# A two-layer graph network on one core: the Newton step of the layer norm on ScalarE, attention emitted earlier, the mean row spread a pair later, one table loaded in disjoint pieces

## The chip, the core and the metric

The kernel runs on one core of a Trainium2 chip. Everything is fp32. The metric is the device time of one execution in microseconds, the median of several. Five engines work side by side, each through its own queue in order, and semaphores hold them together: TensorE (PE; its weight loads PEld), VectorE (DVE), ScalarE (ACT), GpSimd (POOL) and SyncE (SP, which here only issues DMAs). GpSimd issues the indirect DMAs, the gathers and scatters.

## The reference

`x` has 2708 rows of 1024 features; `adj` is a sparse 0/1 matrix of 2708 x 2708 whose first rows have the most ones.

```python
# layer 0
q, k, v = x @ Wq.T + bq, x @ Wk.T + bk, x @ Wv.T + bv
z = (q @ k.T) / sqrt(1024) * adj
z = where(z == 0, -10000, z)
out0 = relu(softmax(z, axis=1) @ v)
x = layernorm(x + out0)            # (t - mean) / sqrt(var + 1e-5)
# layer 1
x = layernorm(x + adj @ (x @ W1) + b1)
```

## The kernel before

**Sparse attention.** Scores are computed at the neighbours of a row only. A first stage (0 to about 134 us) transposes weights, forms M from Wq and Wk, so that a score is x_j . y_i with y = x M, and lists each row's neighbours from `adj`. The rows are then sorted by their number of neighbours into 22 blocks of 128 rows. A record of 28 words a row (neighbours, degree, number of the row) goes through DRAM to the tile `tabs`. The rows of the first 8 blocks (`FAMILY = 8`) are sorted and recorded first, those of the others later. Block 0 holds the rows with most neighbours. The neighbours of its first 32 rows (`HUB`) are dealt over all partitions as shares of a table of their own (the "hub"); its partitions 0 to 31, free by that, take a second share of the neighbours of rows 32 to 63. So `tab0` is block 0's table with 128 records, of which the first 32 rows are overwritten by columns of the next 32 records. `records_out` (L754-772) writes the records and issues these loads on GpSimd's queue: L769, L770, L771, L772.

**The y pairs** (about 134 to 434 us). y for two blocks at a time is formed as seven half products of 8 matmuls each (`half_products`, L308-316) instead of eight, from sums and differences of the operands, in the manner of Strassen. GpSimd forms the sums of x (`y_sums_of`, L395-403, its first is L398). Parts of one pair and the next alternate (`y_pair`, L442).

**Attention** goes on VectorE beside the products: `attend` and `attend_shares` gather neighbour rows of x into a ring of buffers (`gather_slot`, L530, tile `g`), multiply and sum them with y (`score`, L1066), do a running softmax, and sum the rows weighted into `r` (L1125, L1202). For the hub the shares must be joined: a transpose of the maxima (L1210) and a product (L1220) on TensorE.

**The order is partly written out, partly budgeted.** The list `steps` (L1285) has the y steps, then the first layer-0 pair, the step "mean", and nine more pairs. `ahead(i)` (L1396-1436) is called before each step. It finishes what is pending and adds the step's estimated free VectorE time to `credit`: 8.9 for a y step of one block (`HALF_PAIR`), other values from `COST`. While the credit is positive it emits attention jobs from the list `jobs`, each of which draws it down. Within an engine the framework's scheduler then orders the instructions by priority and dependence; `follow` adds a dependence by hand, and evictions of products (`add`, L327-332) have a high priority.

**Layer-0 pairs** (about 434 to 747 us). `turn_pair` (L1232-1245) transposes the two blocks' `r` (`flip`, L978, transposes L985, copies L986) and forms four sums `s_all` on VectorE (L1241-1244). `project_pair` (L1250) multiplies by Wv in seven half products, with bias added at the eviction (L332). `finish_pair` (L1260-1273) applies relu, adds x, and normalizes: `norm` (L1020-1042) does the sum of squares (L1028), logarithm (L1031) and exponential (L1033) on ScalarE, one Newton step for the inverse root on VectorE (L1035, L1036, L1038), minus mean times root (L1040), and then applies both on ScalarE (L1041). `norm_halves` (L1044-1060) is the variant for the last block of a layer. `scatter` (L971-976) writes the rows to `x1_d`. The tiles `t` have two buffers for each place.

**The mean.** The last two blocks, 20 and 21, hold rows without neighbours; their softmax is uniform, so all of them get the mean of x times Wv. `project_mean` (L1003-1018) multiplies, copies four quarters (`quarters`) and spreads them to all partitions by eight matmuls (L1014) into two banks of `p_o`, which the half products use too; `finish0` (L1156-1167) finishes these blocks after the step "mean".

**Layer 1** (about 763 us on). For each row the neighbours' rows of x1 are gathered (L530) and summed on VectorE (L1505, L1508), ten units of two blocks are multiplied by W1, and `norm` and `scatter` to `out` follow. Between the layers are 13 matmuls on data of no use (`WARM`, L1557).

In one call `norm` runs on one block, so 42 calls in a launch: 21 in each layer. The path that computes densely when a check of the lists raises `flag` isn't taken here.

Of the kernel before, what the change touches and what calls it, by code (L numbers as in the profile page):

```python
# [9 lines left out]
F32 = mybir.dt.float32  # L10
# [6 lines left out]
ALU = mybir.AluOpType  # L17
# [4 lines left out]
P = 128  # L22
# [61 lines left out]
def sparse_part(ctx, tc, x, xT, adj, wqT, wkT, wvT, bq, bk, bv, w1, b1, out):  # L84
# [28 lines left out]
    with es:  # L113
# [35 lines left out]
        nc.vector.memset(ones, 1.0)  # L149
        eps = const.tile([P, 1], F32, name="eps")  # L150
        nc.vector.memset(eps, EPS)
        xbT = const.tile([P, DC], F32, name="xbT")
        tabs = const.tile([P, NB, REC], I32, name="tabs")
        degs = const.tile([P, NB], F32, name="degs")
# [169 lines left out]
        def spare_bank():  # L324
            return p_tr.tile([P, 4, P], F32, name="tr").rearrange("p a b -> p (a b)")
# [428 lines left out]
        def records_out(f, nb, rec, pos_i, k0, k1, behind=None):  # L754
            for b in range(k0, k1):
                put = nc.gpsimd.indirect_dma_start(
                    out=tab_ds[f][:, :], out_offset=bass.IndirectOffsetOnAxis(ap=pos_i[:, b:b + 1], axis=0),
                    in_=rec[:, b, :], in_offset=None)
                if behind is not None:
                    follow(put, behind)  # L760
                tc.declare_no_dep(put.ins, group=f"tab{f}", reason="disjoint rows: positions are unique")
                tc.add_to_no_dep_group(f"tab{f}", put.ins)
            if k1 < nb:
                return
            b0 = families[f][0]
            nc.gpsimd.dma_start(out=tabs[:, b0:b0 + nb, :], in_=tab_ds[f].rearrange("(b p) e -> p b e", p=P))
            if f == 0:

                nc.gpsimd.dma_start(out=tab0, in_=tab_ds[0][:P, :])  # L769
                nc.gpsimd.dma_start(out=tab0[:HUB, :J0], in_=tab_ds[0][HUB:2 * HUB, ROW - J0:ROW])  # L770
                nc.gpsimd.dma_start(out=tab0[:HUB, :ROW - J0], in_=tab_ds[0][HUB:2 * HUB, J0:ROW])  # L771
                nc.gpsimd.dma_start(out=tab0[:HUB, ROW:], in_=tab_ds[0][HUB:2 * HUB, ROW:])  # L772
# [230 lines left out]
        def project_mean(w):  # L1003

            acc = p_o.tile([P, HALF], F32, name="po")
            column_tiles(acc, lambda c: xbT[:, c:c + 1].to_broadcast([P, HUB]), w, True)
            quarters = xb_pools[0].tile([P, D // G], F32, name="quarters", bufs=1)
            nc.scalar.copy(quarters, acc[:, :D // G])
            po = []
            for h in range(NH):  # L1010
                acc = p_o.tile([P, HALF], F32, name="po")
                for g in range(h * G // NH, (h + 1) * G // NH):
                    k = g * D // G - h * HALF
                    put = nc.tensor.matmul(acc[:, k:k + D // G], ident[:, g * HUB:g * HUB + 1].to_broadcast([P, P]), quarters,  # L1014
                                           start=True, stop=True)
                po.append(acc)
            products.append(put)
            return po

        def norm(t, sm, n, sm2=None):  # L1020

            nm = stat.tile([P, 1], F32, name="lnm")
            if sm2 is None:
                nc.vector.tensor_scalar_mul(nm[:n], sm[:n], -1.0 / D)
            else:
                nc.vector.tensor_scalar(nm[:n], sm[:n], sm2[:n], -1.0 / D, op0=ALU.add, op1=ALU.mult)  # L1026
            vs = stat.tile([P, 1], F32, name="vs")
            nc.scalar.activation(junks[:n], t[:n], AF.Square, bias=nm[:n], accum_out=vs[:n])  # L1028

            lv = stat.tile([P, 1], F32, name="lv")  # L1030
            nc.scalar.activation(lv[:n], vs[:n], AF.Ln, bias=eps[:n], scale=1.0 / D)  # L1031
            near = stat.tile([P, 1], F32, name="near")
            nc.scalar.activation(near[:n], lv[:n], AF.Exp, scale=-0.5)  # L1033
            ve = stat.tile([P, 1], F32, name="ve")
            nc.vector.scalar_tensor_tensor(ve[:n], vs[:n], D * EPS, near[:n], op0=ALU.add, op1=ALU.mult)  # L1035
            nc.vector.tensor_scalar(ve[:n], ve[:n], near[:n], -0.5 / D, op0=ALU.mult, op1=ALU.mult)  # L1036
            rstd = stat.tile([P, 1], F32, name="rstd")
            nc.vector.scalar_tensor_tensor(rstd[:n], ve[:n], 1.5, near[:n], op0=ALU.add, op1=ALU.mult)  # L1038
            nmr = stat.tile([P, 1], F32, name="nmr")
            end = nc.vector.tensor_tensor(nmr[:n], nm[:n], rstd[:n], op=ALU.mult)  # L1040
            applied.append(nc.scalar.activation(t[:n], t[:n], AF.Identity, bias=nmr[:n], scale=rstd[:n]))  # L1041
            return end

        def norm_halves(t, stats):  # L1044

# [110 lines left out]
        def finish0(b, po, xr):  # L1156
            n = rows[b]
            t = (xb_pools[0] if b == last[-1] else wa).tile([P, D], F32, name="t", bufs=2)
            for h in range(NH):
                hs = slice(h * HALF, (h + 1) * HALF)  # L1160
                with tc.high_priority(URGENT):
                    nc.vector.tensor_add(t[:n, hs], po[h][:n], bias_bc[:n, hs])
            sm = stat.tile([P, 1], F32, name="sm")
            nc.vector.scalar_tensor_tensor(t[:n], t[:n], 0.0, xr[:n], op0=ALU.max, op1=ALU.add, accum_out=sm[:n])
            end = norm(t, sm, n)
            scatter(x1_d[:, :], b, n, t, "x1")
            return end

        def attend_shares(b, got):

# [225 lines left out]
        def ahead(i):  # L1396
            nonlocal credit, pending, wv_t
            kind, b = steps[i]
            for p in pending:
                p[0](*p[1:])  # L1400
                credit -= END * (2 if p[0] is finish_pair else 1)
            pending = []
            credit += COST.get(kind, COST.get(b, HALF_PAIR))
            step[0] = i
            join(i, 3 if left_y else 1)
            if kind == "y" and b == NB - 2:
                (q11, q12), (q21, q22) = wv_q
                follow(nc.vector.tensor_sub(q12, q12, q11), products[-2])
            if kind == "p" and b == pairs[0]:
                (q11, q12), (q21, q22) = wv_q  # L1410
                wv_t = differences()
                nc.vector.tensor_sub(wv_t[0], q22, q12)
                nc.vector.tensor_sub(wv_t[1], wv_t[0], q11)
                nc.vector.tensor_sub(wv_t[2], q21, wv_t[0])
            for c in [c for st in steps[i:i + 3] for c in blocks_of(st) if not left_y and c != 0]:
                while c not in got:
                    credit -= run_job()
            while 0 in jobs and i >= steps.index(("p", (0, 7))) - 3:
                credit -= run_job()
            while jobs and i == len(steps) - 1:  # L1420
                credit -= run_job()
            while jobs and credit > 0 and (jobs[0] in running or len(ring) < RB):
                if not spread and len(jobs) <= late_jobs:
                    break
                credit -= run_job()
            if not left_y:
                turn(i)
            if kind == "y":
                if FAMILY + 1 <= b < FAMILY + 5:
                    next(deal)  # L1430
                if 6 <= b - FAMILY < 11:
                    k0 = 3 * (b - FAMILY - 6)
                    records_out(*later_records, k0, min(k0 + 3, NB - FAMILY), products[-2])
                if b == FAMILY + 11:
                    records_back(1)
                    nc.sync.dma_start(out=bias_bc, in_=bv.to_broadcast([P, D]))

        wv_t = None
        for i, (kind, b) in enumerate(steps):
# [13 lines left out]
                    xb_pools.append(xb_pool)  # L1453
                    xb_bc.append(xb_pool.tile([P, D], F32, name="xb_bc"))
            elif kind == "mean":
                po = project_mean(wv_q)
                pending = [(finish0, b_, po, gather_x(x, b_, b_ == last[-1])) for b_ in last]
            else:
                for k, b_ in enumerate(b):
                    pair_x[b_] = gather_x(x, b_, k)  # L1460
                pending = [(finish_pair, b, project_pair(b, *turned[b]))]
                if i == len(steps) - 4:
                    bcast_rows(u_bc, u_col)
                if i >= len(steps) - 3:
                    row_constants((9, 9, 5)[i - len(steps) + 3])
                if i == len(steps) - 2:
                    for b_ in single:
                        single_scores(b_)
                if b == pairs[0]:
                    bcast_rows(xb_bc[0], xbT)  # L1470
                    spread.append(b)
# [440 lines left out]
```

## Time and profile before

| | |
|---|---|
| median of three runs | 1063.62 us (1061.48, 1063.62, 1068.64) |
| the profiled execution, own time | 1064.65 us |
| its span in the trace | 1062.8 us |
| TensorE busy | 957.9 us, 2675 matmuls |
| VectorE busy | 863.9 us |
| ScalarE busy | 420.9 us |
| GpSimd busy | 600.3 us |
| moved by DMA | 229.23 MB |

"Busy" counts the time in which an engine executes something; the rest of the span it waits or issues. In lines of the waits view the columns are: engine, what waits and its line, after the arrow the engine or DMA whose result came last, then microseconds in total, times, and the longest. In lines of a timeline: start, length, engine, line, operation, number of instructions in the row, and in brackets the engine's idle time before it with what ended that. In lines of the groups view: line, engine, operation, out and in with their shapes, count, busy time, mean nanoseconds of one, and the idle time before. "L1041" is line 1041 of the kernel before.

### The profile page before, as it was taken

Reading aid. Unit: us, or ns where it says so; the run is one execution under the profiler, and the core shown is the slowest. Engines: PE = TensorE matmul, PEld = TensorE weight load, DVE = VectorE, ACT = ScalarE, POOL = GpSimd, SP = SyncE. Lnnn points to the kernel's source line nnn. Section 1 sums busy time; section 2 is a strip of 40 time slices with the busy share of each in tenths; the row PEclk is TensorE's granted clock in tenths of the full one; section 3 lists DMA queues with packets and bytes.
Section 4 is the critical chain, followed back from the end, with each engine's and each line's share of the span. In section 5 each row is a group of like instructions: output and inputs, shape, how many; then the busy total and the mean of one; then the engine's idle time right before and its main releaser. Section 6 shows DMA issues by size and latency. Waiting matters only on the chain.

```text
span 1062.8 us, 10517 instructions
## 1 busy us (share of the span) xinstructions
PE 957.9 (90%) x2675; PEld 451.1 (42%) x2675; DVE 863.9 (81%) x2035; ACT 420.9 (40%) x932; POOL 600.3 (56%) x479
## 2 busy tenths in 40 slices
PE   8889999699968999897899989997799999989894
PEld 6334344244423444353454444443344444535341
DVE  8999997587677878899889989996668877869632
ACT  4633536463342434231442454431421343352621
POOL 4841043243677784445656666783587777768510
PEclk9989999899989899898999999998899999999998
DMA  9456679346777578554844897899597599987731
GB/s 358 150 178 182 195 223 288 108 148 216 165 232 230 172 225 283 190 157 124 239 149 114 246 259 211 289 320 357 183 303 189 200 318 283 326 239 220 210 107 43
DMA packets 106093, 229.23 MB, mean 216 GB/s; under 512 B 20014, under 2 KB 47414, under 8 KB 106024
## 3 DMA queue, kind: packets, MB, share of 16 engines
q0 software_dynamic: 51152, 159.06, 49.4%
q1 hardware_dynamic: 54872, 69.42, 20.2%
q8 instruction: 23, 0.38, 0.1%
q14 instruction: 46, 0.38, 0.1%
HBM read 218.10 MB, written 33.64 MB: 237 GB/s over the span
## 4 chain that ended last, share of the span: by engine, by line
PE 29%; DVE 26%; issue 18%; DMA 14%; POOL 9%; ACT 2%; SPq 0%; POOLq 0%; DVEq 0%; ACTq 0%
PE po L310 22%; PE tr L310 5%; DVE junkv L1066 5%; POOL g L530 3%; DMA g<-x_d,tabs 3%; DVE r L1125 3%; DMA g<-in_x_dram,tabs 3%; DVE t L332 2%; DVE at_a L239 2%; DMA wv<-in_wvT_dram 2%; POOL xr L514 1%; DMA xr<-x_d,tabs 1%; DMA x_d<-t,tabs 1%; POOL g L514 1%; DMA g<-x_d,tab 1%
## 5 line engine op out<-in xcount | busy, mean ns | idle before, releaser
L310 PE MATMUL po<-t,s_all 128*128 128x512 f32 x320 | 153.4, 623 | 11.3 <-DVE xr L332 6.0
L530 POOL DMA_INDIRECT g<-in_x_dram,tabs x84 | 109.8, 1307 | 56.9 <-issue 14.2
L1066 DVE SCALAR_TENSOR_TENSOR junkv<-yg,g 128x1024 uint8<-128x1024 f32 x84 | 107.0, 1274 | 20.3 <-DMA yg<-y_d,tabs 8.9
L1508 DVE SCALAR_TENSOR_TENSOR r<-g,valid,r 128x1024 f32<-128x1024 f32 x77 | 98.2, 1281 | 18.6 <-DMA g<-x_d,tabs 15.9
L310 PEld LDWEIGHTS po<-t,s_all 128*128 128x128 f32 x320 | 62.7, 199 | 92.6 <-issue 72.0
L310 PE MATMUL po<-wv,s_all 128*128 128x512 f32 x160 | 77.4, 623 | 16.8 <-DVE s_all L1241 9.5
L530 POOL DMA_INDIRECT g<-x_d,tabs x66 | 77.4, 1173 | 24.7 <-issue 14.9
L1125 DVE SCALAR_TENSOR_TENSOR r<-g,pr,r 128x1024 f32<-128x1024 f32 x64 | 86.0, 1344 | 5.6 <-ACT r L1123 5.0
L310 PE MATMUL po<-y_t,xt 128*128 128x512 f32 x160 | 77.2, 629 | 14.8 <-DVE yo L332 14.1
L310 PE MATMUL po<-y_t,y_s 128*128 128x512 f32 x160 | 74.0, 606 | 13.0 <-POOL y_s L398 13.0
L239 DVE FIND_INDEX8 at_a<-ones,a 128x8 uint16<-128x83 f32 (+3 forms) x132 | 82.1, 630 | 0.2 <-issue 0.2
L1041 ACT ACTIVATE t<-t,nmr,rstd 128x1024 f32<-128x1024 f32 (+1 forms) x40 | 49.3, 1238 | 78.6 <-DVE nmr L1040 62.8
L1028 ACT ACTIVATE junks<-t,lnm 128x1024 uint8<-128x1024 f32 (+1 forms) x40 | 45.9, 1146 | 80.6 <-DVE lnm L1026 77.4
L310 PE MATMUL po<-w,rT 128*128 128x512 f32 x160 | 75.3, 613 | 2.6 <-DVE t L1545 2.5
L310 PE MATMUL po<-t,rT 128*128 128x512 f32 x160 | 74.5, 605 | 1.6 <-DVE t L332 1.6
L255 ACT ACTIVATE junk<-a 128x2756 uint8<-128x2756 uint32 (+1 forms) x22 | 55.0, 2502 | 45.1 <-issue 30.6
L310 PE MATMUL po<-w,s_all 128*128 128x512 f32 x160 | 72.3, 593 | 0.0
L310 PE MATMUL po<-wv,rT 128*128 128x512 f32 x160 | 71.5, 597 | 0.0
L508 ACT ACTIVATE junka<-xt 128x128 uint8<-128x128 f32 x168 | 51.8, 308 | 46.3 <-PE po L310 32.8
L986 ACT COPY rT<-tr 128x512 f32<-128x512 f32 x76 | 41.4, 584 | 70.9 <-PE tr L985 46.4
L310 PEld LDWEIGHTS po<-y_t,xt 128*128 128x128 f32 x160 | 31.8, 202 | 57.0 <-issue 37.4
L310 PEld LDWEIGHTS po<-wv,s_all 128*128 128x128 f32 x160 | 31.3, 201 | 56.4 <-issue 34.7
(415 smaller groups left out, 1904.6 us busy)
## 6 DMA issues: line engine op xcount, KB each, us to landing
xt<-in_xT_dram SPq DMA_DIRECT2D x21, 512.0 KB
y_d<-yo SPq DMA_DIRECT2D x42, 256.0 KB
a<-in_adj_dram SPq DMA_DIRECT2D x21, 413.5 KB
a<-in_adj_dram SPq DMA_DIRECT2D x21, 338.5 KB
a<-in_adj_dram SPq DMA_DIRECT2D x21, 263.5 KB
wq_i<-in_wqT_dram SPq DMA_DIRECT2D x8, 512.0 KB
wk_i<-in_wkT_dram SPq DMA_DIRECT2D x8, 512.0 KB
wv<-in_wvT_dram SPq DMA_DIRECT2D x16, 256.0 KB
```

The lines of the kernel that those rows point to most:

```text
L239: nc.vector.max_index(at[:n, i], ones[:n, :8], a[:n, cuts[i] + 8 * i:cuts[i + 1] + 8 * i + 8])
L255: put = nc.scalar.activation(junk[:n], loaded[b][:n, :AW].bitcast(U32), AF.Sign, accum_out=cnt[:n, b:b + 1])
L310: put = nc.tensor.matmul(acc, a[:, k], w[:, k], start=start and k == 0, stop=stop and k == DC // 2 - 1, skip_group_check=True)
L332: nc.vector.tensor_add(to, acc, what)
L508: put = nc.scalar.activation(junka[:, :xt.shape[2]], xt[:, c, :], AF.Copy, scale=of_first if c < DC // 2 else 1.0, accum_out=xs[:, c, b:b ...
L530: nc.gpsimd.indirect_dma_start(out=dst[:n], out_offset=None, in_=src, in_offset=bass.IndirectOffsetOnAxis(ap=at, axis=0), bounds_check=N - ...
L986: nc.scalar.copy(rT[:, g * 4:g * 4 + 4, :], tr)
L1028: nc.scalar.activation(junks[:n], t[:n], AF.Square, bias=nm[:n], accum_out=vs[:n])
L1041: applied.append(nc.scalar.activation(t[:n], t[:n], AF.Identity, bias=nmr[:n], scale=rstd[:n]))
L1066: put = nc.vector.scalar_tensor_tensor(junkv[:n], yg[:n], scale, xg[:n], op0=ALU.mult, op1=ALU.mult, accum_out=s)
L1125: nc.vector.scalar_tensor_tensor(r[:n], xg[j][:n], pr[:n, j:j + 1], r[:n], op0=ALU.mult, op1=ALU.add)
L1508: put = nc.vector.scalar_tensor_tensor(r[:n], xg[:n], ok[:n, j:j + 1], r[:n], op0=ALU.mult, op1=ALU.add)
```

## The change

Five edits.

1. Block 0's table is loaded into partitions 32 to 127 only, so that it no longer covers the 32 rows that the next loads write.
2. `norm` does its Newton step on ScalarE: four VectorE instructions are replaced by five activations with per-partition scale or bias, with two constant tiles, set once, for -0.5 eps and 1.5. The values are grouped otherwise: (-0.5/D vs - 0.5 eps) near^2 + 1.5, times near.
3. `project_mean` returns the quarters; the eight spreading matmuls are a function of their own, which is hung behind the sixth half product from there on (`between`), and write to banks from the transposes' pool instead of `p_o`. The last two blocks are finished after the pair (4, 3) instead of after "mean".
4. The credit of the last six y steps (b from 14 to 19) is 1.7 larger.
5. The return values of `norm` and `finish0`, which nothing uses, are gone.

```diff
--- before.py
+++ after.py
+        half_eps, three_halves = [const.tile([P, 1], F32, name=name) for name in ("half_eps", "three_halves")]
+        nc.vector.memset(half_eps, -0.5 * EPS)
+        nc.vector.memset(three_halves, 1.5)
...
             if f == 0:
 
-                nc.gpsimd.dma_start(out=tab0, in_=tab_ds[0][:P, :])
+                nc.gpsimd.dma_start(out=tab0[HUB:], in_=tab_ds[0][HUB:P, :])
                 nc.gpsimd.dma_start(out=tab0[:HUB, :J0], in_=tab_ds[0][HUB:2 * HUB, ROW - J0:ROW])
                 nc.gpsimd.dma_start(out=tab0[:HUB, :ROW - J0], in_=tab_ds[0][HUB:2 * HUB, J0:ROW])
                 nc.gpsimd.dma_start(out=tab0[:HUB, ROW:], in_=tab_ds[0][HUB:2 * HUB, ROW:])
...
             nc.scalar.copy(quarters, acc[:, :D // G])
+            return quarters
+
+        def spread_mean(quarters, behind):
+
             po = []
             for h in range(NH):
-                acc = p_o.tile([P, HALF], F32, name="po")
+                acc = spare_bank()
                 for g in range(h * G // NH, (h + 1) * G // NH):
                     k = g * D // G - h * HALF
                     put = nc.tensor.matmul(acc[:, k:k + D // G], ident[:, g * HUB:g * HUB + 1].to_broadcast([P, P]), quarters,
                                            start=True, stop=True)
+                    follow(put, behind, same=True)
                 po.append(acc)
-            products.append(put)
             return po
...
             nc.scalar.activation(near[:n], lv[:n], AF.Exp, scale=-0.5)
+            nc.scalar.activation(vs[:n], vs[:n], AF.Identity, bias=half_eps[:n], scale=-0.5 / D)
+            nc.scalar.activation(lv[:n], near[:n], AF.Square)
             ve = stat.tile([P, 1], F32, name="ve")
-            nc.vector.scalar_tensor_tensor(ve[:n], vs[:n], D * EPS, near[:n], op0=ALU.add, op1=ALU.mult)
-            nc.vector.tensor_scalar(ve[:n], ve[:n], near[:n], -0.5 / D, op0=ALU.mult, op1=ALU.mult)
+            nc.scalar.activation(ve[:n], lv[:n], AF.Identity, bias=three_halves[:n], scale=vs[:n])
             rstd = stat.tile([P, 1], F32, name="rstd")
-            nc.vector.scalar_tensor_tensor(rstd[:n], ve[:n], 1.5, near[:n], op0=ALU.add, op1=ALU.mult)
+            nc.scalar.activation(rstd[:n], near[:n], AF.Copy, scale=ve[:n])
             nmr = stat.tile([P, 1], F32, name="nmr")
-            end = nc.vector.tensor_tensor(nmr[:n], nm[:n], rstd[:n], op=ALU.mult)
+            nc.scalar.activation(nmr[:n], nm[:n], AF.Copy, scale=rstd[:n])
             applied.append(nc.scalar.activation(t[:n], t[:n], AF.Identity, bias=nmr[:n], scale=rstd[:n]))
-            return end
...
-            credit += COST.get(kind, COST.get(b, HALF_PAIR))
+            credit += COST.get(kind, COST.get(b, HALF_PAIR + (1.7 if kind == "y" and b >= FAMILY + 6 else 0)))
...
             elif kind == "mean":
-                po = project_mean(wv_q)
-                pending = [(finish0, b_, po, gather_x(x, b_, b_ == last[-1])) for b_ in last]
+                quarters, po = project_mean(wv_q), []
+                between[len(began) + 6] = [lambda put: po.extend(spread_mean(quarters, put))]
             else:
                 for k, b_ in enumerate(b):
                     pair_x[b_] = gather_x(x, b_, k)
                 pending = [(finish_pair, b, project_pair(b, *turned[b]))]
+                if b == pairs[1]:
+                    pending += [(finish0, b_, po, gather_x(x, b_, b_ == last[-1])) for b_ in last]
```

More of the change, by code (lines that the diff above doesn't have):

```diff
@@ L1164, in finish0 @@
             nc.vector.scalar_tensor_tensor(t[:n], t[:n], 0.0, xr[:n], op0=ALU.max, op1=ALU.add, accum_out=sm[:n])
-            end = norm(t, sm, n)
+            norm(t, sm, n)
             scatter(x1_d[:, :], b, n, t, "x1")
-            return end
         def attend_shares(b, got):
```

## The prediction

> **What bounds the kernel now.** I read the engine totals first, then the digits by slice, then the engine waits, and then the timelines at those places where TensorE stands still.
>
> ```profile
> span 1062.8 us, 10517 instructions
> PE 957.9 (90%) x2675; PEld 451.1 (42%) x2675; DVE 863.9 (81%) x2035; ACT 420.9 (40%) x932; POOL 600.3 (56%) x479
> PE   8889999699968999897899989997799999989894
> ...
> DVE  8999997587677878899889989996668877869632
> ```
>
> TensorE is busy 90% of the span, VectorE 81%. The stage view (25 us each) splits this: from 175 to 200 VectorE works 13.2 of 25 us, from 450 to 700 it works 24.9, 23.7, 24.9, 18.7, 25.0, 25.0, 24.1, 22.4, 25.0 and 25.0, and in layer 1 about 19 to 20. So in the ten layer-0 pairs two engines are nearly full at once, and a VectorE microsecond counts there; in layer 1 it doesn't. What can be won is TensorE's standing time, so I look at who ends it.
>
> ```profile
> PE po L310 <- POOL y_s L398: 13.0, 2, 10.6
> PE po L310 <- DVE s_all L1241: 9.5, 3, 5.3
> DVE t L332 <- DMA x_d<-t,tabs: 12.5, 3, 8.3
> ACT t L1041 <- DVE nmr L1040: 62.8, 22, 15.8
> POOL x_d L972 <- ACT t L1041: 33.2, 9, 6.8
> ...
> 195.92 2.07 PE L310 MATMUL po<-y_t,y_s 128*128 128x512 f32 x2 [10.61 <-POOL y_s L398]
> ...
> 447.87 2.07 PE L310 MATMUL po<-wv,s_all 128*128 128x512 f32 x2 [5.28 <-DVE s_all L1241]
> ...
> 731.55 4.79 PE L310 MATMUL po<-wv,s_all 128*128 128x512 f32 x6 [7.33 <-DVE t L332]
> ```
>
> The first five are waits (total, times, longest), the last three are TensorE's timeline with the gap ahead in brackets. One y product waits 10.61 us for GpSimd; the first pair waits 5.28 us for its second operand; the last but one stretch waits 7.33 us for an addition that itself waits for a scatter. Later gaps of the pairs, from the same timeline: 3.91, 0.77, 1.57, 4.00 (to 529.29), 0.45, 2.65.
>
> ```profile
> 183.58 0.57 POOL L769 DMA_DIRECT2D tab<-tab_d  x1
> 184.46 1.02 POOL L514 DMA_INDIRECT rec_r<-tab_d,r_i  x1 [0.30 <-issue]
> 188.49 0.55 POOL L770 DMA_DIRECT2D tab<-tab_d  x1 [3.01 <-DMA tab<-tab_d]
> 189.03 0.50 POOL L772 DMA_DIRECT2D tab<-tab_d  x1
> 194.08 0.50 POOL L771 DMA_DIRECT2D tab<-tab_d  x1 [4.55 <-DMA tab<-tab_d]
> 194.59 1.27 POOL L398 TENSOR_TENSOR y_s<-xt 128x512 f32<-128x512 f32 x1
> ```
>
> This is the cause of the 10.61: GpSimd's queue holds y_s behind two waits, each for the landing of the table load before it, because the loads overlap in the tile.
>
> ```profile
> L1031 ACT ACTIVATE lv<-vs,eps 128x1 f32<-128x1 f32 x40 | 11.7, 294 | 0.6
> L1033 ACT ACTIVATE near<-lv 128x1 f32<-128x1 f32 x40 | 8.0, 200 | 0.8
> L1035 DVE SCALAR_TENSOR_TENSOR ve<-vs,near 128x1 f32<-128x1 f32 x40 | 6.2, 154 | 7.5 <-ACT near L1033 7.1
> L1036 DVE TENSOR_SCALAR ve<-ve,near 128x1 f32<-128x1 f32 x40 | 8.4, 209 | 0.4
> ...
> 716.60 1.24 ACT L1041 ACTIVATE t<-t,nmr,rstd 128x1024 f32<-128x1024 f32 x1 [0.87 <-DVE nmr L1040]
> ```
>
> The Newton step's VectorE operations are 0.15 to 0.21 us each; what is long is their turn in the queue. The near of the last line's block ended at 711.05 on ScalarE, its application began at 716.60: 5.55 us for a step of 0.67 us.
>
> **What the Trainium skill says.** "ScalarE: Activation LUTs", What ACT_TABLE_LOAD costs: an activation with immediate scale and bias takes 186 ns plus 0.833 ns an element, each per-partition operand adds about 93 ns. The trace agrees: 200 ns without such an operand (L1033), 294 with one (L1031), 1238 for 1024 elements with two (L1041; by the page 1225). "TensorE: Matmul & The Clock Gate", Part 1: after about 3.4 us of idleness the clock falls to half until some 3.4 us of work have passed. Here the first eight products after the stalls that end at 195.92, 447.87, 529.29 and 731.55 take 5.52, 5.84, 5.40 and 5.65 us instead of 8 x 0.43 = 3.43: about 2 us that go with the stall. "DMA: Bandwidth & Descriptors", Anatomy of one DMA: some 2 us of a DMA are fixed, mostly the confirmation of the last byte. The table loads take longer here: L769 ended its issue at 184.15 and released L770 at 188.49 (4.34), L770 released L771 5.04 after its own issue.
>
> **The change part by part**, against the profiled execution (1064.65 us; span 1062.8 and 1.85 around it). It lies 1.03 above the median of the runs, 1063.62, inside their scatter of 1061.5 to 1068.6.
>
> *Table in disjoint loads.* The 96-row load and the first column load no longer overlap, so the latter needn't wait; the third, whose columns overlap the second's, still does. It can start at 184.15 + 0.55 + 5.04 = 189.7 instead of 194.08, and y_s follows: -4.4. The ends: -5.1 with the landing of 4.34, -3 if two loads in flight slow each other. From 196 to 279 TensorE runs without a gap of 2 us, so the gain is carried. The stall stays above 3.4 us, so no warm clock is won.
>
> *More attention (credit +1.7 on six y steps, 10.2 us in all).* The rewritten order of instructions shows eleven more attention operations on VectorE between L1408, the differences of Wv, and the first pair's s_all. Priced by the rows (1.2 to 1.3 us a wide operation, 0.1 a tiny one) the queue between is 42.4 us where it was 26.4; before, it took 29.8, 3.4 of them idle. It now starts at 417.37 - 4.4 = 413.0 and, with some 4.6 idle for gathers, gives s_all at 460.0 where it was 447.1 and TensorE began at 447.87. So the first pair is 12.1 later. In return the later pairs find their operands made: the gaps 3.91 + 0.77 + 1.57 + 4.00 and two warm-ups of 2 go, 14.3 in all, and 24 transposes (8 of the mean row's, 16 of the second pair; 0.28 each by L985, 6.8) stand ahead of the first pair's s_all products instead of behind them: they fill the wait, and I count half, 3.4, since some have sources that are late too. Net 12.1 - 14.3 - 3.4 = -5.6 at the second half of the third pair, of which -4.4 is the table's. Idle for gathers may lie between 0 and 21 (a gather took 7.5 from issue to use; three of them), so the net is between -10.2 and +10.8. The ring has eight buffers and gathers already run ahead, which is why I stay low.
>
> *Newton on ScalarE.* Taken away: 4 x 42 VectorE operations, 0.67 us by durations and 0.4 by queue places, as they overlap: 8.6 us for layer 0's 21. Added: five activations of 0.29, 0.20, 0.39, 0.29, 0.29 = 1.47 us, 62 in all on an engine that is busy 421 of 1063; beside the products they are hidden. Without cover an eviction on ScalarE behind such a chain is 1.5 later. The application at 716.60 can begin at 711.05 + 1.47 = 712.5, 4.1 earlier, and its scatter with it; the 7.33 gap falls to 3.2 and 2 of warm-up go: -6.1. The ends: 0, as the DMAs are 99% busy there and the landing may not move; -9.3 if the gap closes. The small gaps 0.45 and 2.65 give about -1. In layer 1 VectorE has five idle microseconds in 25: 0, between -3 and +3.
>
> *The layer boundary.* TensorE waits 7.75 us for the first gathers of x1, that is for the last pair's scatters. In the new order the halved last application stands behind the other block's whole ScalarE chain (1.47) and half of its application (0.6): +2, between 0 and +4. At the very end the same is covered by ScalarE's 3.7 idle us.
>
> *Mean and rest.* The spread products (8 x 0.38) move into transposes' banks a few products later, the two last blocks' finish a pair later; work and traffic stay the same, and their price is in the 4.00 gap above. Two memsets and a swap of a store with a weight load on SP: 0.
>
> Sum: -5.6 - 6.1 - 1 + 2 = -10.7, or **1054.0** on the profiled time; the runs lie about 1 lower, so I predict **1053**.
>
> **Rivals.**
> A. *VectorE is the true bound of the pairs.* The windows of 25.0 speak for it. Then its relief counts whole: 4.4 + 8.6 and the 8.32 idle before L332, less 2: -19.3, 1045. Against it: TensorE is also at 25.0 in several windows.
> B. *Only the table's gain arrives.* The first pair's delay just balances the returned gaps (4.4 net), and the last scatter isn't sooner because the transfers are full: 1064.65 - 4.4 = 1060, and the small terms cancel. For it: the DMA share of 0.99 from 700 to 725.
> C. *The first pair's operand comes too late: slower.* Place: s_all L1241 behind the attention put ahead of it, TensorE waiting in order, first at the hub's transpose, then at s_all. By the terms above the time is 1064.65 + (s_all - 470.7): from s_all at 471 on the change loses. Three gathers late by 7.5 put it at 477, so 1071. For it: VectorE already stood 3.4 us in this stretch, and L530's gathers wait on ScalarE and VectorE; against it: eight buffers.
> D. *The disjoint load does nothing*, since the remaining overlap still costs a landing and two transfers in flight are slower: -6.6, 1058.
>
> **How the numbers follow.** Forecast 0.42 (own range 1048 to 1058), A 0.24, B 0.17, C 0.12, D 0.05. A measurement of this kernel tells about 1% from no change, 10.6 us, so faster means below 1053.0. Forecast gives 0.24 of its chance to faster (its centre is at the bound, but the queue relief in the pairs is counted low) and 0.18 to same; A all to faster; B and D to same, as does 0.02 of C. Faster 0.48, same 0.42, slower 0.10. The range, 1041 to 1066, takes in A's centre and leaves out most of C.
>
> **What would show it.** Right: the stall before the first y_s falls to about 6 us, and GpSimd has one wait for a table landing, not two; TensorE waits for the hub's transpose and s_all together 15 to 20 us before the first pair, then hardly until 700; the waits of L1041's successor on VectorE vanish (62.8 us before); the gap near 724 is below 4; the boundary gap is 8 to 10. The prediction is wrong if s_all comes after 471, if the application's wait only turns into a wait for ScalarE's own queue, or if layer 1 changes by more than 3 us.

## The result, and the profile after

The changed kernel takes 1067.67 us (median), the one before 1061.87 in the same series; the ratio is 1.0047, 95% interval [1.0027, 1.0067]. So it is half a per cent slower, some 5 us, where 1053 was forecast with a range of 1041 to 1066. In what follows a ratio against the kernel before is turned into microseconds with 1061.

The page after, its first lines and engine totals:

```profile
span 1066.0 us, 10579 instructions
PE 961.6 (90%) x2675; PEld 451.8 (42%) x2675; DVE 855.2 (80%) x1869; ACT 464.8 (44%) x1142; POOL 616.8 (58%) x479
```

VectorE lost 166 instructions and 8.7 us, ScalarE gained 210 and 43.9 us, TensorE has the same 2675 matmuls and was busy 3.7 us longer. TensorE's timeline after, the lines with a long gap (in brackets) ahead of them; lines of the code are 3 to 8 higher than before:

```profile
190.62 6.70 PE L313 MATMUL po<-y_t,y_s 128*128 128x512 f32 x8 [5.03 <-POOL y_s L401]
...
397.65 5.40 PE L313 MATMUL po<-y_t,xt 128*128 128x512 f32 x8 [3.52 <-DVE yo L335]
...
443.87 0.47 PE L1216 MATMUL tr<-ident,nm 128*128 128x128 f32 x1 [9.57 <-DVE nm L1195]
...
464.49 6.31 PE L313 MATMUL po<-wv,s_all 128*128 128x512 f32 x8 [6.10 <-DVE s_all L1247]
...
665.33 1.94 PE L988 MATMUL tr<-ident,r 128*128 128x128 f32 x8 [5.48 <-DVE r L1132]
...
738.74 5.72 PE L313 MATMUL po<-wv,s_all 128*128 128x512 f32 x8 [5.00 <-DVE t L335]
...
765.06 1.06 PE L988 MATMUL tr<-ident,r 128*128 128x128 f32 x8 [2.58 <-DVE r L1513]
```

Read it from the top against the lines of before. The product at y_s starts 5.3 earlier (190.62 for 195.92). Then a gap of 3.52 appears at 397.65 that wasn't there. The last y product begins at 427.27, before at 426.87: the gain is gone before the pairs begin. The first pair's s_all products start at 464.49, 16.6 later than before (447.87), behind two waits. In the pairs the gap before the last but one stretch is still 5.00, and a new one of 5.48 stands at 665. Layer 1 begins 2.1 later than before and ends 3.2 later.

GpSimd's timeline at the table, after:

```profile
183.72 0.59 POOL L772 DMA_DIRECT2D tab<-tab_d  x1
184.29 0.53 POOL L773 DMA_DIRECT2D tab<-tab_d  x1
184.78 0.54 POOL L775 DMA_DIRECT2D tab<-tab_d  x1
185.62 1.03 POOL L517 DMA_INDIRECT rec_r<-tab_d,r_i  x1 [0.30 <-issue]
188.75 0.53 POOL L774 DMA_DIRECT2D tab<-tab_d  x1 [2.10 <-DMA tab<-tab_d]
189.29 1.27 POOL L401 TENSOR_TENSOR y_s<-xt 128x512 f32<-128x512 f32 x1
```

One wait for a landing is left of two, as the diff says. The groups of the norm, after (line, engine, operation, busy us, mean ns, idle before):

```profile
L1044 ACT ACTIVATE ve<-lv,three_halves,vs 128x1 f32<-128x1 f32 x40 | 15.1, 378 | 0.5
L1048 ACT ACTIVATE nmr<-lnm,rstd 128x1 f32<-128x1 f32 x40 | 11.6, 290 | 0.6
...
L1049 ACT ACTIVATE t<-t,nmr,rstd 128x1024 f32<-128x1024 f32 x39 | 48.2, 1236 | 0.6
```

The application (L1041 before, L1049 now) waited 78.6 us in all before, of that 62.8 for VectorE; now 0.6. That wait has vanished entirely, and the kernel is slower.

### The profile page after: what moved, and what is told of

It is laid out like the page before. It is cut to its first block, busy times and chain, and to the rows that moved or that the text cites. A ratio compares the mean times of both kernels' runs of the same rounds, so it can differ in the third digit from the quotient of the medians.

```text
span 1066.0 us, 10579 instructions
## 1 busy us (share of the span) xinstructions
PE 961.6 (90%) x2675; PEld 451.8 (42%) x2675; DVE 855.2 (80%) x1869; ACT 464.8 (44%) x1142; POOL 616.8 (58%) x479
## 4 chain that ended last, share of the span: by engine, by line
DVE 28%; PE 23%; issue 20%; DMA 15%; POOL 9%; ACT 3%; SPq 1%; POOLq 0%; DVEq 0%; ACTq 0%
PE po L313 20%; DVE at_a L242 5%; DMA g<-in_x_dram,tabs 4%; DVE r L1132 4%; POOL g L533 4%; DVE junkv L1073 3%; DVE t L335 2%; DMA g<-x_d,tabs 2%; DMA xt<-in_xT_dram 2%; POOL tab_d L759 1%; DMA a<-in_adj_dram 1%; DMA yg<-y_d,tabs 1%; PE tr L988 1%; DMA xr<-x_d,tabs 1%; DVE t L1272 1%
## 5 line engine op out<-in xcount | busy, mean ns | idle before, releaser
L313 PE MATMUL po<-t,s_all 128*128 128x512 f32 x320 | 148.8, 608 | 8.5 <-DVE xr L335 5.6
L533 POOL DMA_INDIRECT g<-in_x_dram,tabs x84 | 113.1, 1347 | 54.5 <-ACT r L1130 17.0
L313 PE MATMUL po<-y_t,xt 128*128 128x512 f32 x160 | 77.7, 631 | 16.6 <-DVE yo L335 15.8
L313 PE MATMUL po<-wv,rT 128*128 128x512 f32 x160 | 74.0, 612 | 0.0
L335 DVE TENSOR_TENSOR xr<-po,xr 128x512 f32<-128x512 f32 x31 | 21.3, 688 | 40.8 <-PE po L313 16.6
```

Source lines behind the costliest of these rows:

```text
L313: put = nc.tensor.matmul(acc, a[:, k], w[:, k], start=start and k == 0, stop=stop and k == DC // 2 - 1, skip_group_check=True)
L335: nc.vector.tensor_add(to, acc, what)
L533: nc.gpsimd.indirect_dma_start(out=dst[:n], out_offset=None, in_=src, in_offset=bass.IndirectOffsetOnAxis(ap=at, axis=0), bounds_check=N - ...
```

## Experiments

Names: T is the disjoint table load, M the mean's edit, C the extra credit, N the Newton step on ScalarE. The changed kernel is T+M+C+N.

**One part undone at a time.** First without the credit:

```diff
-            credit += COST.get(kind, COST.get(b, HALF_PAIR + (1.7 if kind == "y" and b >= FAMILY + 6 else 0)))
+            credit += COST.get(kind, COST.get(b, HALF_PAIR))
```

> The changed kernel without the 1.7 of extra credit. Theory 1 (attention put ahead of the first pair is what loses: after, TensorE stood 9.57 us for the hub's maxima and 6.10 for s_all where it had stood 5.28): the first pair starts near 443 and the time is 6 to 10 below the changed kernel, 1057 to 1062. Theory 2 (the Newton step on ScalarE loses): the loss stays, within 3 of the changed kernel's 1067.7. Theory 3 (the later spread of the mean loses): within 3 likewise.

Measured: 1072.73, ratio 1.0101 [1.0058, 1.0143]. It is slower still, by more than any of the three theories allowed, though the first pair's s_all products now start at 442.02 instead of 464.49. So the late first pair, which theory 1 blamed, isn't what makes the changed kernel slower than the one before: theory 1 falls.

Without the Newton step on ScalarE (the four VectorE instructions put back):

> The changed kernel with the Newton step back on VectorE. Theory 1: VectorE has 8.6 us more queue in the pairs again, so no faster than the changed kernel, up to 6 slower (1067 to 1074). Theory 2: ScalarE's chains of 1.5 us are what holds scatters, gathers and evictions, so it is 5 or more faster, 1058 to 1063. Theory 3: no change, 1067.

Measured: 1057.89, ratio 0.9963 [0.9946, 0.9980]. The time is that of theory 2: N costs 8.9 us here (1.0047 - 0.9963). Whether it costs by ScalarE's chains, as the theory says, this run doesn't tell.

Without the disjoint table:

> The changed kernel with the whole-table load that overlaps the others. Theory 1: the 5.6 us at y_s come back at 195 us but are absorbed before the y phase ends, as the gain was (both kernels' last y product starts at 429.4): within 2 of the changed kernel's 1067.7. Rival: the gain was carried and only covered by another loss: 5 slower, 1072 to 1074.

Measured: 1073.54, ratio 1.0119 [1.0079, 1.0160]. The table's load is worth 7.6 us at the end (1.0119 - 1.0047; six runs, so the interval is wide), so it isn't absorbed; the rival's reading is right. The order of instructions on TensorE, VectorE and ScalarE is that of the changed kernel, so here only the load differs.

Without the mean's edit (spread at once, into `p_o`, the last blocks finished after "mean"):

> The changed kernel with the mean's row spread in the product banks at once and the two last blocks finished a step earlier, as before. Theory 1: within 3 of the changed kernel, 1065 to 1071; the wait of an addition for a scatter near 529 (3.7 us) comes back. Theory 3: 4 or more faster, below 1064.

Measured: 1062.85, ratio 1.0016 [0.9997, 1.0035]. Beside N, M seems to cost 3.3 us by the ratios and 4.8 by the medians, about what theory 3 gave (4 or more), but the two intervals overlap.

**Where the Newton step loses.** `norm` gets a flag for the engine, and the calls of one layer pass it:

```diff
-        def norm(t, sm, n, sm2=None):
+        def norm(t, sm, n, sm2=None, on_scalar=True):
```

> The changed kernel with the Newton step on ScalarE in layer 0 only, on VectorE in layer 1. The changed kernel took 1067.7, the one with all steps on VectorE 1057.9. Theory 2a (the loss of the step on ScalarE is in the pairs, where TensorE had gaps of 2.0, 5.5 and others between 505 and 730 which the other kernel hasn't): near the changed kernel, 1064 to 1068. Theory 2b (the loss is in layer 1 and at the boundary): near 1058 to 1060.

> The changed kernel with the Newton step on ScalarE in layer 1 only. Theory 2a: 1058 to 1061. Theory 2b: 1064 to 1068.

Measured: layer 0 only 1064.90, ratio 1.0036 [1.0019, 1.0054]; layer 1 only 1058.70, ratio 0.9974 [0.9957, 0.9992]. Against 0.9963 with none on ScalarE that is 7.7 us for layer 0 and about 1 for layer 1. Theory 2a.

**Table and credit without the two others:**

> The kernel before with the disjoint table and the extra credit alone. From the runs that undo one part: without the Newton step on ScalarE 9.8 less than the changed kernel, without the mean's edit 4.8 less. If the parts add up, 1053; if the mean's edit loses only together with the Newton step (its order of TensorE's work), 1058, as without that step alone.

Measured: 1060.13, ratio 0.9990 [0.9973, 1.0007]. The parts don't add up: M gains 3 us here (0.9963 with it), where beside N it lost 3. Either figure is hardly clear of the intervals; their difference is.

**ScalarE's time, VectorE's relief, or the order.** The step left out, so that four of the five activations go:

```diff
+            rstd = near
             nmr = stat.tile([P, 1], F32, name="nmr")
             nc.scalar.activation(nmr[:n], nm[:n], AF.Copy, scale=rstd[:n])
```

> The changed kernel with the Newton step left out: the exponential is used as the inverse root, and one activation forms minus mean times root; so four activations of some 1.2 us a block are gone and none is put on VectorE. Theory 2c (the activations' time on ScalarE, ahead of scatters, copies and gathers, is the loss): 1058 or below, as with the step on VectorE. Theory 2d (the loss is the order into which the kernel falls when VectorE is relieved: attention and transposes are placed by the budget and the scheduler, and then wait for gathers): it stays at 1064 to 1068.

Measured: 1058.62, ratio 0.9982 [0.9960, 1.0003]. VectorE is relieved as in the changed kernel, ScalarE has one activation more a norm than before, and the time is that of the step on VectorE (0.9963) within the intervals. That fits 2c; it also says that the relief I counted on brings nothing measurable in this kernel.

Then the burden without the relief, and the burden put on the kernel without the step (there with `range(3)`):

```diff
+            spare = stat.tile([P, 1], F32, name="spare")
+            nc.scalar.activation(spare[:n], near[:n], AF.Identity, bias=half_eps[:n], scale=-0.5 / D)
+            for _ in range(4):
+                nc.scalar.activation(spare[:n], near[:n], AF.Identity, bias=three_halves[:n], scale=spare[:n])
```

> The changed kernel with the Newton step on VectorE, and between the exponential and the application five further activations of one element a partition whose result nobody reads. VectorE has all its old work. The kernel without these five took 1057.9. Theory 2c (the activations' own time on ScalarE, 1.5 us a block ahead of the scatters, copies and evictions, is the loss): 1063 to 1068, the loss comes back without any relief of VectorE. Theory 2e (the loss is the order that the scheduler happened to build): anywhere, but as likely 1058 as more; within 2 of 1058 would speak against 2c.

> The kernel with the Newton step left out (1058.6) and four activations of one element a partition in its place whose result nobody reads, so with ScalarE's load of the changed kernel but a shorter chain. Theory 2c: 1064 to 1069. If only the chain's length counts (the application can't start before the last of five that depend on each other), and the added ones still stand ahead of it in the queue, it is the same; theory 2e: near 1058 as likely as not.

Measured: 1061.01, ratio 0.9991 [0.9972, 1.0010], so 3.0 us over 0.9963; and 1063.48, ratio 1.0012 [0.9994, 1.0030], 3.2 us over 0.9982. So a burden on ScalarE comes with a third of the 8.9, though these activations take more time than N's: 1.81 us a norm for five (0.287 + 4 x 0.380) against 1.42. The instructions on TensorE and VectorE also stand in another order in each of these kernels than in the one it is compared with, so even this third is not ScalarE's time for certain.

**Table and mean alone, and a mend of the first pair:**

> The disjoint table and the mean's edit alone, no extra credit and no Newton step on ScalarE. Table, mean and credit together took 1057.9. If the credit is worth 5 here too, as it was beside the Newton step: 1063. If its gain was tied to ScalarE's chains: 1055 to 1058, since the first pair then waits some 5 us instead of 16 for the hub's maxima and s_all.

Measured: 1048.22, ratio 0.9866 [0.9837, 0.9896]. This is 13 us below the kernel before (1061.07 in this series), 14 by the ratio. So the credit costs 10.3 us without N (0.9963 against 0.9866), and N costs 24.9 without the credit (1.0101 against 0.9866).

```diff
-                if i >= entry[1] + least:
+                if i >= entry[1] + least and not (entry[0] == "hub" and i <= steps.index(("p", pairs[0]))):
...
+            with tc.high_priority(URGENT):
                 nc.vector.tensor_add(S[0], a21, a22)
```

> Table, mean and credit without the Newton step on ScalarE (1057.9), with two mends for the first pair: the hub's join isn't emitted until the first pair's products are, and the four s_all sums have the evictions' priority. TensorE stood 10.05 us for the hub's maxima and 6.09 for s_all. If these waits set the end: they fall to some 4, the attention delayed is 2.7 us a pair, and the time is 1048 to 1053. If VectorE's queue sets it anyway, the time only moves to later waits: 1056 to 1059.

Measured: 1066.22, ratio 1.0045 [1.0029, 1.0061], 8.7 us slower than without the mend. TensorE's timeline of this kernel at the first pair:

```profile
444.78 1.11 PE L988 MATMUL tr<-ident,r 128*128 128x128 f32 x4 [9.22 <-ACT rT L989]
445.68 9.18 PE L313 MATMUL po<-wv,rT 128*128 128x512 f32 x16
454.70 3.60 PE L313 MATMUL po<-wv,s_all 128*128 128x512 f32 x8
```

The s_all products do start earlier, at 454.70 instead of 467.40, but one wait has turned into another (9.22 for a copy on ScalarE), and the order of the later pairs is another one too; neither expectation was right.

**Each part alone, and single loads on the best kernel.** M alone and T+M have the same order of instructions on TensorE, VectorE and ScalarE; only GpSimd's differs, at the table loads. The same holds for the kernel before and T alone, but for two memsets on VectorE.

> The kernel before with the disjoint table load alone; the orders of TensorE, VectorE and ScalarE stay those of before. Table and mean together took 1048.2, before 1061.1. If y_s's 4 to 6 us at 195 us reach the end: 1055 to 1057. If they are absorbed: 1060 to 1062.

> The kernel before with the mean's edit alone; its orders on TensorE, VectorE and ScalarE are those of table and mean together (1048.2), so what differs is the stall at y_s. If the parts add: table -5, so mean -8 and this 1053. If the mean's edit is all: 1048 to 1049.

Measured: T 1055.29, ratio 0.9946 [0.9923, 0.9969]; M 1053.27, ratio 0.9930 [0.9903, 0.9956]. In microseconds T is -5.7, M -7.4, both -14.2 by ratio: without C and N the two add up. M, for which I had counted nothing beyond one gap, gains no less than T by these intervals. What it takes away is waits of additions for scatters, the very thing that N was to shorten. Between the first and the last product of the pairs VectorE waited 12.5 us for that before, 12.4 with T alone, and 0.3 with M alone (T first, then M):

```profile
DVE t L335 <- DMA x_d<-t,tabs: 12.4, 4, 7.8
DVE t L335 <- DMA x_d<-t,tabs: 0.3, 1, 0.3
```

The gap of 7.33 before the last but one stretch is 7.65 with T alone; with M alone two small ones stand there, 0.21 and 1.26. Why the later finish of the last two blocks does this was not tested; the order of the pairs changes with it.

> Table and mean (1048.2), and five further activations of one element a partition in each norm ahead of the application, read by nobody. ScalarE's time alone cost 3.1 and 4.9 in the two other pairs of runs. If it is that here too: 1051 to 1054. If most of the 24.5 us that the Newton step on ScalarE costs without the credit is ScalarE's time: 1062 to 1072.

> Table and mean with the Newton step left out: the exponential is used as the inverse root and one activation forms minus mean times root. VectorE is relieved, ScalarE's chain grows by one activation. If the relief of VectorE is worth its 8.6 us of queue: 1040 to 1044. If it is worth nothing because gathers and order decide: 1047 to 1052. If the order that follows from the relief is what loses: above 1057.

Measured: the five unread activations 1052.30, ratio 0.9919 [0.9893, 0.9945], 5.6 us over T+M; the step left out 1055.24, ratio 0.9938 [0.9918, 0.9959], 7.6 us over T+M. The kernel that relieves VectorE didn't gain, it lost, more than its expectation for "nothing" and less than that for a loss by order; here too the order is another one. Putting the four chained activations into that kernel gives T+M+N, 1.0101: another 17 us.

**The rest of the table's stall, and layer 1.**

> Table and mean (1048.2), with the Newton step on ScalarE in layer 1 only; layer 0's order is unchanged. If the loss is in the pairs: 1047 to 1051. If layer 1's path is sensitive too: above 1053.

Measured: 1048.55, ratio 0.9870 [0.9835, 0.9904], equal to T+M. So, by subtraction, all of N's 24.9 us are in layer 0.

```diff
-                nc.gpsimd.dma_start(out=tab0[:HUB, :J0], in_=tab_ds[0][HUB:2 * HUB, ROW - J0:ROW])
+                nc.gpsimd.dma_start(out=tab0[:HUB, ROW - J0:J0], in_=tab_ds[0][HUB:2 * HUB, 2 * (ROW - J0):ROW])
```

> Table and mean, with the second table load cut to the columns that the third doesn't write (9 to 15 instead of 0 to 15), so that no load waits for another. The stall at y_s, 6.1 us in that kernel's trace, falls to 1 to 2. With the same orders on TensorE, VectorE and ScalarE a gain at y_s reached the end one for one (mean alone against mean and table: 5 us): so 1043 to 1045. If what is left of the stall is covered by the next wait: 1047 to 1048.

Measured: 1043.07, ratio 0.9819 [0.9778, 0.9861]. It is the fastest kernel of all, 19 us below the one before. GpSimd's timeline of this kernel:

```profile
184.67 0.52 POOL L773 DMA_DIRECT2D tab<-tab_d  x1
185.16 0.52 POOL L774 DMA_DIRECT2D tab<-tab_d  x1
185.65 0.53 POOL L775 DMA_DIRECT2D tab<-tab_d  x1
186.49 1.03 POOL L517 DMA_INDIRECT rec_r<-tab_d,r_i  x1 [0.30 <-issue]
187.52 1.29 POOL L401 TENSOR_TENSOR y_s<-xt 128x512 f32<-128x512 f32 x1
```

No load waits for another, and y_s starts at 187.52 (194.59 before). TensorE's gap there:

```profile
188.87 3.70 PE L313 MATMUL po<-y_t,y_s 128*128 128x512 f32 x8 [2.23 <-POOL y_s L401]
```

The gap is 2.23 and the eight products after it take 3.70, where they take 5.52 in the kernel before and 6.70 in the changed one. A gap of this length doesn't always spare them: in the changed kernel eight products after a gap of 1.99 (at 626.53) take 5.40. The medians differ by 5.2 us from T+M; the two intervals overlap slightly at 0.986, so the gain's size is less certain than its direction.

## Why the prediction was wrong

**The table (step 1): right.** -4.4 forecast; y_s's product came 5.3 earlier, and the end 5.7 (T alone), 6.8 (beside M) and 7.6 (beside the three others) earlier, each time with the order on the other engines unchanged. I had written that the warm clock isn't won back; in the changed kernel that is so (6.70 for eight products after a gap of 5.03).

**The extra attention (step 2): wrong, twice.** I had s_all at 460.0; it came at 463.75. (Three gathers of 7.5 us are 22.5, not 21, so the upper end of that term should have been +12.3.) More important, I priced only VectorE's queue from L1408 on. The credit acts from y step 14, and beside those steps it puts a gap of its own: 3.52 at 397.65 (3.4 to 3.5 at that place in each of the other profiles with the credit, no such gap in those without). In single profiles the last y product starts at 421.56 with T alone and at 429.14 with T+C; so in the y phase C cost as much as T had gained. VectorE at that place in the changed kernel:

```profile
394.53 2.46 DVE L1127 TENSOR_SCALAR r<-r,turn 128x1024 f32<-128x1024 f32 x1
396.92 0.68 DVE L335 TENSOR_TENSOR yo<-po,yo 128x512 f32<-128x512 f32 x1
```

The eviction of the y product stands behind attention in VectorE's queue. The second error is the return: I counted 17.7 us given back by the third pair. The first pair's s_all products were 16.6 late, the third pair's second products (535.40 for 529.29) 6.1 late: 10.5 came back, with N in the kernel too. The credit as a whole costs 4.7 us on T and 10.3 on T+M; beside N it gains 5.7, which shows that its value is no constant.

**The Newton step (step 3): wrong in sign; this is the step that failed the forecast.** The term was -6.1 for the gap at 724 and -1 for small gaps; the runs show +8.9 in this kernel and +24.9 without the credit, all in layer 0. The other parts together (T+M+C, 0.9963) came to -3.9 where -5.6 was forecast, but by luck: on T's -5.7, M brings -8.5 and C +10.3, where C and M's gap together had been counted at -1.2.

The price of the activations was right: 0.28, 0.19, 0.38, 0.29 and 0.29 us, 1.42 together for 1.47 forecast, and ScalarE's busy time rose by 43.9 rather than 62 because successive ones overlap in the records (one near ends at 731.54 where the next activation begins at 731.45). The formula of "ScalarE: Activation LUTs", What ACT_TABLE_LOAD costs, holds for each of them. Three things around them were wrong:

First, I took a waiting time for a cost. L1041 waited 62.8 us for VectorE in all, and I followed only one of these waits to what stands behind it. At that one, the gap of 7.33, I let the scatter move forward with the application. GpSimd's queue in the kernel before doesn't allow that:

```profile
717.11 2.03 POOL L514 DMA_INDIRECT g<-y_d,tabs  x1 [0.30 <-issue]
719.44 1.02 POOL L972 DMA_INDIRECT x_d<-t,tabs  x1 [0.30 <-issue]
```

The scatter was issued at 719.44, 1.60 after its application had ended (717.84), and GpSimd had issued one transfer after another since 708.33, with 0.30 us between them. With this order an application 4.1 earlier leaves the scatter where it is, and the addition that waited for it began only at 730.81, 11.4 after its issue. In the runs it was M that closed the gap. In the changed kernel, with N's order, the gap is 5.00, and the addition that ends it (L335 at 738.00) stands in VectorE's queue behind operations that wait for gathers, not for a scatter:

```profile
732.13 1.22 DVE L1332 SCALAR_TENSOR_TENSOR junkv<-g,part 128x1024 uint8<-128x1024 f32 x1 [1.82 <-DMA g<-in_x_dram,tabs]
...
736.84 1.23 DVE L1332 SCALAR_TENSOR_TENSOR junkv<-g,part 128x1024 uint8<-128x1024 f32 x1 [0.75 <-DMA g<-in_x_dram,tabs]
...
738.00 0.69 DVE L335 TENSOR_TENSOR t<-po,bias_bc 128x512 f32<-128x512 f32 x1
```

Second, I held that a VectorE microsecond counts in the pairs, because VectorE is busy for 25.0 of 25 us there; rival A counted 8.6 us of relief whole. From the first s_all products to the last product of the pairs, the single profiles show this (us):

| | stretch | VectorE busy | VectorE idle |
|---|---|---|---|
| T+M+C | 275.82 | 262.10 | 13.72 |
| the changed kernel, T+M+C+N | 286.67 | 258.12 | 28.55 |
| T+M | 293.00 | 278.62 | 14.38 |
| T+M+N | 315.20 | 274.85 | 40.35 |

N takes some 4 us of work from VectorE, and VectorE then stands idle 14.8 and 26.0 us longer. So the relief was lost: what VectorE would have done next wasn't there yet. Part of what it waits for are gathers. The waits in the stretch of the pairs, for T+M+N (442 to 771) first:

```profile
DVE junkv L1073 <- DMA yg<-y_d,tabs: 11.4, 3, 4.9
DVE junkv L1073 <- DMA g<-in_x_dram,tabs: 9.2, 5, 3.0
```

and for T+M (446 to 755):

```profile
DVE junkv L1072 <- DMA g<-in_x_dram,tabs: 1.5, 2, 1.0
DVE junkv L1072 <- DMA yg<-y_d,tabs: 1.2, 1, 1.2
```

The score operations wait 20.6 us for gathers of y and x where they waited 2.7. In the changed kernel against T+M+C the difference is smaller: 5.5 us and one wait of 5.56 for which the profile names no cause, against 5.8. That one wait stands behind the new gap of 5.48 on TensorE at 665.33:

```profile
660.35 1.23 DVE L1073 SCALAR_TENSOR_TENSOR junkv<-yg,g 128x1024 uint8<-128x1024 f32 x1 [5.56 <-issue]
...
663.90 1.28 DVE L1132 SCALAR_TENSOR_TENSOR r<-g,pr,r 128x1024 f32<-128x1024 f32 x1
```

Why the gathers come later is not shown. A gather of y rows lands on a copy that ScalarE makes, so a longer queue on ScalarE could delay it; but GpSimd's waits for these copies fell with N, from 13.3 us (T+M) to some 5 (T+M+N). Its waits for ScalarE's weighted rows (L1130; L1129 with T+M), before gathers of x, rose from 4.7 to 11.2.

Third, I had put a further load on ScalarE at nothing, from its 40%. The three pairs of runs with unread activations differ by 3.0 to 5.6 us, with other orders.

**What stays open.** Of N's 24.9 us on T+M, 7.6 came with the step left out and 5.6 with the unread activations; if these add, some 12 are left. None of it was separated from the order of instructions, which on TensorE and VectorE changed in every kernel with N in layer 0, with the step left out, or with unread activations. The orders alone, with the same work, differ by as much: C reorders and costs 10.3 or gains 5.7, the mend of the first pair reorders and costs 8.7. No run held the order fixed and changed only N. So that N in layer 0 is what costs is shown; whether it costs by its time and its dependent chain on ScalarE or by the order that comes with it is not.

**Mean and rest: mis-sized.** Counted as part of the 4.00 gap; alone it gives 7.4 us, and 8.5 on T. Beside N it seems to lose 3.3.

**Boundary: wrong in sign.** +2 forecast. The last pair's last products end 7.2 later than before (751.16 for 743.91), and the wait there fell from 7.75 to 2.58, so layer 1 began only 2.1 later. Layer 1 itself: 300.9 us for 299.8, inside my 3.

Of the rivals, C named the first pair's late s_all as the way to a loss. The loss came, but not by that mechanism: s_all was ahead of its threshold of 471, and without C the kernel is slower still. A falls with the idle time of VectorE above, D with the 5.7 us that T gains alone.

Of the signs that I had named, these came: one landing wait, a stall of 5.03 before the first y_s, 15.7 us of waiting before the first pair, and no wait of the application. These did not: a gap below 4 near 724 (5.00), hardly a wait until 700 (5.48 at 665), a boundary gap of 8 to 10 (2.58).

## What to carry to other kernels

A large sum of waits on an engine pair says nothing of gain until it is followed to what stands late behind it: here 62.8 us of waiting went, and the time rose. Before work is moved from a full engine to a half-empty one, ask whether the first one's next work is there: here VectorE had some 4 us less to do in the pairs and stood idle 14.8 us longer. Follow each result through the in-order queues that lie behind it, here GpSimd's, where the scatter had its place. And a bundle should be measured part by part: two of these four edits gave 13 us, and one more load cut to fit gave 5, while the other two took all of the 13 away and 5 more.

## What was not expected of the hardware

Two loads in flight into different rows of a tile were not slower than one after the other. From the end of a load's issue to the issue of the load that waits for it, the sixteen profiles with T as in the change, where the 96-row load is in flight as well, show 3.07 to 5.96 us (3.93 in the changed kernel). The three without T (before, M alone, the changed kernel without T) show 4.34, 3.05 and 4.93 for the first wait and 5.04, 5.16 and 4.81 for the second. With no overlap left the y sums started 7.1 us earlier than before.
